# A graph network's first pair: filter taps of three outputs in two row groups of TensorE, and gates that begin with x and messages

## The chip, the core and the metric

The kernel runs on one core of one Trainium2 chip. The metric is the device time of one execution in microseconds, as the median of repeated runs. TensorE (PE, with its weight loads PEld) does the matrix products, VectorE (DVE), ScalarE (ACT) and GpSimd (POOL) the elementwise work, and SyncE (SP) issues nearly all DMA transfers. Every engine works through its own queue in order.

## The reference

There are 64 graphs of 256 nodes with 256 features each, all in fp32, and two layers. The first layer has a convolution branch of 17 taps along the nodes, a message branch and a gated unit that joins them:

```python
h = relu(bn1(conv1(xc)))                       # 1 tap, xc is x transposed
x_conv = relu(bn2(conv2(h)) + xc)              # 17 taps, 256 -> 256 channels
s = x @ w_se.T + b_se                          # 3 numbers per node
A = exp(-dist(s, s)) * adj
x_nmp = A @ relu(x @ w_msg.T + b_msg)          # messages
gi, gh = [x_conv, x_nmp] @ w_ih.T + b_ih, x @ w_hh.T + b_hh
r, z = sigmoid(gi_r + gh_r), sigmoid(gi_z + gh_z)
x = layernorm(x + (1 - z) * tanh(gi_n + r * gh_n) + z * x)
# layer 1
hn = layer_norm(x, gamma, beta)
x = layernorm(x + relu((adj @ hn) @ W_rel + b_rel + hn @ W_root))
```

## The kernel before

**Pairs and blocks.** Graphs are worked on in 32 pairs. Eight graphs, four pairs, share one block of the convolution. The convolution of 17 taps is a product of polynomials: DVE splits the inputs into 47 (`NM`) frequencies (`split_all`, `split_u`, `butterflies`, L679), TensorE multiplies each frequency by its own 256 x 256 matrix (`product`, L707), and DVE puts the results together again (`merges`, then L897 to L905), after which ACT scales them into `xc` (`kept`, L911). All of block b+1 is spread over the pairs of block b.

**The filters.** The 47 matrices `W2` are made at the start from the 17 taps of `conv2_w`, in `filters()`. Before the change POOL lays seven output channels (`OB = 7`) of 17 taps side by side in `ws` (`laid`, L542, one copy for four such blocks), TensorE transposes each block (`turned`, L548), ACT copies the result to `tT` (L550), TensorE multiplies it by a constant matrix `taps` of 119 rows and 329 columns (L565), and ACT writes the 329 columns to `W2` (L568), each with seven outputs of all 47 frequencies. The ring `ws` is four groups deep. Every frequency needs all outputs, so block 0's products (`products_added`, `last_products`) begin only when the filters are done. `W2` is stored to DRAM for the later blocks (`store_w2`), and the pool that holds it closes after block 0's last product. The gates' weights `WB` are loaded into the space that is then free (L1026).

**A pair.** `pair(p)` computes the messages (`ps_msg`, L1092, and L1095 which adds the bias in pairs 0 and 1 by a product of one row), the distances (`ps_dist`, L1125: four products of four rows each in row groups of their own and in four banks), the adjacency-weighted exponentials, the sum of the messages `nmp` (`ps_nmp`, L1139), adds x to `xc` (L1145, L1146), and then the gates. A gate bank holds 512 columns: half for r or z, half for a part of n. Most pairs use a form with seven products in place of eight; pairs 0, 1 and the last, `PLAIN`, use eight plain ones into `ps_g`. For pairs 0 and 1 a bank takes its eight products in two groups, one for each half of the features; each group takes x, xc and messages in this order:

```python
for f in range(C):
    for g in gs:
        a = bank("ps_g", "gate")
        for k in range(C):
            product(a, (f, k, g), T is ZN, k == 0)
        put(T, f, g, a)
```

Four of the eight PSUM banks may be held for gates, six for the rest. After the gates come the first norm, the projection (`ps_hy`, L1311), the aggregation (`ps_agg`, L1325), the last norm and the store.

**Small sums.** `beta`, two tiles of 128 columns, is made by DVE (L1042) and multiplied by the layer's weights (`ps_hrow`, L1045); the column means of the weights follow (`ps_mean`, L1054).

**The x loads.** From block 3 on (`TURN_FROM`) x is loaded in 32 x 32 blocks with a DMA for every four blocks (L799, sixteen DMAs for a pair), so that DVE can transpose it (L813).

**The order.** Every operation has a key, a due time. `scheduled()` plays the program with estimated durations and takes, for each engine, the ready operation with the smallest key; the order that comes out is each engine's queue. DVE operations of a pair get `PAIR_LEAD` taken from their keys. `FIRST_GATES` is the due time of pair 0's gates, `PERIOD` the step from pair to pair, `GATE_TIME` the time for half of the gates; `spread` gives the convolution and the filters keys between two times.

Of the kernel before, what the change touches and what calls it, by code (L numbers as in the profile page):

```python
# [18 lines left out]
P = 128  # L19
B, N, D = 64, 256, 256  # L20
C = D // P
# [30 lines left out]
NM = 3 * len(LEAVES) + 2  # L52
SR, LR = 32, 100
SQ = 32
OB = 7
HQ = 2 * M * C * (M + 1)
XC_SLOTS = BG + 2
FIRST_GATES, PERIOD, GATE_TIME = 143.0, 60.5, 17.0
AHEAD_FROM, AHEAD_TO, W_DEEP = -20.0, 10.0, 2
CONV1_FROM, CONV1_TO, CONV_FROM, CONV_OUT, CONV_TO = -10.0, 120.0, -6.0, -70.0, -30.0  # L60
PAIR_LEAD, FILTER_LEAD, LOAD_AHEAD = 20.0, 15.0, 12.0
SMALL_RUNS, TURN_FROM = 2.5, 3
PLAIN, SUMS_FROM = (0, 1, B // 2 - 1), 2


# [199 lines left out]
class Engine:  # L265
# [4 lines left out]
    def __getattr__(self, method):  # L270
        program, name = self.program, self.name

        def call(*args, hold=(), need=(), lines_up=0, **named):
# [12 lines left out]
            if method == "dma_start":  # L286
                v = outs[0] if isinstance(outs[0], View) else named["in_"]
                dur, moved = 0.06, v.size() * v.at.shape[0] * 4
                if program.joined is not None:
                    moved *= SMALL_RUNS  # L290
            elif name == "tensor":
                turned = method == "transpose" or named.get("is_transpose")
                dur = 0.109 if turned else 2 * max(0.109, n * 0.8333e-3 + 0.0025)
            elif name == "vector":
                dur = 0.182 if method == "bn_aggr" else 0.147 + 1.044e-3 * (args[1].size() if method == "bn_stats" else n)
                dur += 0.06 * (method == "scalar_tensor_tensor" and isinstance(args[2], View))
            elif name == "scalar":
                dur = 0.16 + 0.83e-3 * n + 0.11 * sum(isinstance(named.get(k), View) for k in ("bias", "scale"))
                dur += 0.2 * ("accum_out" in named)
                where = outs[0].at[0].ravel()  # L300
                dur += 0.9e-3 * n * (n > 1 and "accum_out" not in named and where[1] - where[0] > 1)
            else:
                dur = 1.5 if ALU.pow in args else 0.45 + 1.5e-3 * n
# [106 lines left out]
def gnn_two_layers(  # L410
# [65 lines left out]
    h_dram = tc.dram_tile([B // 2, 5, P, D], F32, name="hd")  # L476
    xt_dram = tc.dram_tile([B // 2, P, C, 2 * N], F32, name="xt")
    W2 = sb("w2all", [P, C, NM, D], "first")
    taps = sb("taps", [TAPS * OB, NM * OB], "filters")

    prog.at(0.0)
    A.dma_start(out=chan_sb, in_=chan)
    A.dma_start(out=w1, in_=w1T.rearrange("(c p) n -> p c n", p=P))
    tb = np.einsum("kf,op->kofp", tap_matrix(), np.eye(OB, dtype=np.float32)).reshape(TAPS * OB, NM * OB)
    A.dma_start(out=taps, in_=nc.inline_tensor(np.ascontiguousarray(tb), name="tap_matrix").ap())
    V.memset(mhalf, -0.5)
    V.memset(ones, 1.0)
# [25 lines left out]
            SP.dma_start(out=w2m[f:g, c].rearrange("f p o -> p f o"), in_=W2[:, c, f:g, :])  # L513

    def filters():
        pieces, groups = [], []
        for c in range(C):
            for o0, o1 in ((0, 12 * OB), (12 * OB, 24 * OB), (24 * OB, D)):
                starts = [min(o, D - OB) for o in range(o0, o1, OB)]
                for a in range(0, len(starts), 4):  # L520
                    groups.append((len(pieces), starts[a:a + 4]))
                pieces.append((c, o0, o1))
        WT, TT = {}, {}
        WS, AHEAD = {}, 4
        wts = ring("wt", [P, TAPS, D - 24 * OB], 2, "filters")
        wss = ring("ws", [P, 4, TAPS, OB], AHEAD, "filters")
        tTs = ring("tT", [TAPS * OB, 4, P], 2, "filters")

        def fetch(i):
            if i < len(pieces):  # L530
                c, o0, o1 = pieces[i]
                t = next(wts).rearrange("p k o -> p (k o)")[:, :TAPS * (o1 - o0)]
                WT[i] = t.rearrange("p (k o) -> p k o", k=TAPS)
                SP.dma_start(out=WT[i], in_=w2T[c, :, :, o0:o1])

        def laid(i):
            piece, starts = groups[i]
            n, o = len(starts), starts[0] - pieces[piece][1]
            if i == 0 or groups[i - 1][0] != piece:
                fetch(piece + 1)  # L540
            WS[i] = next(wss)
            G.tensor_copy(WS[i][:, :n], WT[piece][:, :, o:o + n * OB].rearrange("p k (b o) -> p b k o", o=OB))  # L542

        def turned(i):
            ps, n = bank("ps_tT"), len(groups[i][1])
            with prog.group():
                for k in range(n):
                    PE.transpose(ps[:TAPS * OB, k * P:(k + 1) * P], WS[i][:, k].rearrange("p k o -> p (k o)"), ident)  # L548
            tT = next(tTs)
            A.copy(tT[:, :n].rearrange("k b p -> k (b p)"), ps[:TAPS * OB, :n * P])  # L550
            return tT

        fetch(0)
        for i in range(AHEAD):
            laid(i)
        TT[0] = turned(0)
        for i, (piece, starts) in enumerate(groups):
            c = pieces[piece][0]
            if i + AHEAD < len(groups):
                laid(i + AHEAD)  # L560
            if i + 1 < len(groups):
                TT[i + 1] = turned(i + 1)
            for a, o in enumerate(starts):
                ps = bank("ps_w")
                PE.matmul(ps[:, :NM * OB], TT[i][:, a, :], taps, start=True, stop=True)  # L565
                skip = OB - D % OB if o == D - OB else 0
                pv = ps[:, :NM * OB].rearrange("p (f o) -> p f o", o=OB)
                A.copy(W2[:, c, :, o + skip:o + OB], pv[:, :, skip:])  # L568

    def sl(a, n, step=1):  # L570
        return X[:, a:a + n] if step == 1 else X[:, a:a + (n - 1) * step + 1:step]
# [212 lines left out]
    def conv1(b):  # L784
# [5 lines left out]
        def fetch(g):  # L790
            if b >= TURN_FROM:
                XN[g] = xn_ahead[:, :4 * D]
                blocks = XN[g].rearrange("p (c g b i) -> p g c b i", c=C, g=2, i=SQ)
                with prog.group():
                    for a in range(P // SQ):
                        for k in range(2):
                            for c in range(C):
                                at = c * P + a * SQ
                                SP.dma_start(out=blocks[a * SQ:(a + 1) * SQ, k, c], in_=x[b * BG + g + k][  # L799
                                    :, at:at + SQ].rearrange("(b j) i -> j b i", j=SQ))  # L800
                return
            if b > 0:
                XN[g] = xn_ahead[:, :4 * D].rearrange("p (j d) -> p j d", d=D)
# [134 lines left out]
    prog.lead = 0.0  # L938
    at3 = len(prog.ops)
    spread(at1, at2, 2.0, 14.0)  # L940
    spread(at2, at3, 12.0, 70.0)
    for o in prog.ops[at1:at3]:
        if o.moved:
            o.key = min(o.key, 20.0)
# [41 lines left out]
    G.tensor_sub(half_r, half_r, bhh[:, 2])  # L986
    G.tensor_scalar(half_r, half_r, 0.5, None, ALU.mult)

    prog.at(58.0, 0.01)
    store_w2(0)  # L990
    store_w2(1)

# [46 lines left out]
    beta = HY[:, 0, 0, :D].rearrange("p (c e) -> p c e", c=C)  # L1039
    ps = bank("ps_hrow")  # L1040
    for c in range(C):
        V.tensor_scalar(beta[:, c, :], ones, gb[:, 1, c:c + 1], None, ALU.mult)  # L1042
    with prog.group():
        for c in range(C):
            PE.matmul(ps, beta[:, c, :], wrr[:, c, :], start=(c == 0), stop=(c == C - 1))  # L1045
# [23 lines left out]
    def pair(p):  # L1069
# [79 lines left out]
        for v, t, when in zip(ins, (tx, nmps, tc_), (due - 28, due - 10, due - 20)):  # L1149
# [16 lines left out]
                V.tensor_sub(t3, b22, b12)  # L1166
            right.append((b11, b21, b22, t4, t1, t2, t3))

        def product(ps, i, second, start):
            gates = (((0, (0, 2, 1)), (2, (0,))), ((1, (0, 2, 1)), (2, (2, 1))))[second]  # L1170
            left, at = i, i
# [31 lines left out]
        if plain:  # L1203
            prog.at(due, 2 * GATE_TIME / 44)
            for gs in ((0,), (1,)) if apart else ((0, 1),):
                for T in (RG, ZN):
                    for f in range(C):
                        for g in gs:
                            a = bank("ps_g", "gate")
                            for k in range(C):  # L1210
                                product(a, (f, k, g), T is ZN, k == 0)
                            put(T, f, g, a)
                        squash(T, f, gs)
        else:
# [258 lines left out]
```

## Time and profile before

| | |
|---|---|
| median of 3 runs | 2065.92 us (2064.77 to 2066.36) |
| the profiled execution | 2065.45 us |
| its span, first to last instruction | 2063.7 us |
| granted TensorE clock, mean | 0.995 |
| PE, DVE, ACT, POOL busy | 98%, 81%, 51%, 14% |
| chain that ended last, by engine | PE 92%, DVE 5% |
| tap matmuls L565 | 24.0 to 72.0 us from the start |
| pair 0's gates, first `ps_g` matmul | 152.1 us |

The profile is of one execution. Its line for a group of instructions has the source line, engine, operation, tiles, shapes and count, then the busy time and the mean of one, then the idle time ahead of them and what ended it. An fp32 matmul appears as two MATMUL rows, so 74 tap matmuls are counted as 148. A table by stretches gives, for each stretch, the busy time and count of PE, PEld, DVE, ACT and POOL, then the granted clock (1.00 is full speed), the share of the DMA engines that was busy and the GB/s.

### The profile page before, as it was taken

Reading aid. Unit: us, or ns where it says so; the run is one execution under the profiler, and the core shown is the slowest. Engines: PE = TensorE matmul, PEld = TensorE weight load, DVE = VectorE, ACT = ScalarE, POOL = GpSimd, SP = SyncE. Lnnn points to the kernel's source line nnn. Section 1 sums busy time; section 2 is a strip of 40 time slices with the busy share of each in tenths; the row PEclk is TensorE's granted clock in tenths of the full one; section 3 lists DMA queues with packets and bytes.
Section 4 is the critical chain, followed back from the end, with each engine's and each line's share of the span. In section 5 each row is a group of like instructions: output and inputs, shape, how many; then the busy total and the mean of one; then the engine's idle time right before and its main releaser. Section 6 shows DMA issues by size and latency. Waiting matters only on the chain.

```text
span 2063.7 us, 28744 instructions
## 1 busy us (share of the span) xinstructions
PE 2029.6 (98%) x10332; PEld 1645.4 (80%) x10332; DVE 1678.4 (81%) x2587; ACT 1047.5 (51%) x2460; POOL 296.9 (14%) x520
## 2 busy tenths in 40 slices
PE   9989999999999999999999999999999999999997
PEld 6868779778887788877887778877888778887875
DVE  7983798899968998889968998799887899875644
ACT  7453534754446544565447544475445554465432
POOL 4010210111111111101101121112110111111100
PEclk9999999999999999999999999999999999999999
DMA  8834363334433264334532354333452224211100
GB/s 213 265 99 156 105 205 121 105 120 146 152 97 113 78 184 138 95 100 125 176 98 97 101 155 149 104 116 84 151 159 80 72 77 153 93 38 61 41 21 31
DMA packets 284683, 241.21 MB, mean 117 GB/s; under 512 B 110469, under 2 KB 269180, under 8 KB 284540
## 3 DMA queue, kind: packets, MB, share of 16 engines
q1 hardware_dynamic: 283998, 238.94, 37.8%
q8 instruction: 82, 1.34, 0.3%
q14 instruction: 61, 0.50, 0.1%
q10 hardware_dynamic: 542, 0.43, 0.1%
HBM read 177.85 MB, written 61.47 MB: 116 GB/s over the span
## 4 chain that ended last, share of the span: by engine, by line
PE 92%; DVE 5%; ACT 1%; issue 1%; POOL 0%; POOLq 0%; DVEq 0%; ACTq 0%
PE ps_a L1179 21%; PE ps_k L707 15%; PE ps_hy L1311 10%; PE ps_d L1179 10%; PE ps_msg L1092 5%; PE ps_agg L1325 5%; PE ps_b L1179 5%; PE ps_nmp L1139 5%; PE ps_c L847 5%; PE ps_g L1179 4%; PE ps_w L565 2%; PE ps_wT L1276 1%; DVE XF L679 1%; PE ps_dist L1125 1%; PE ps_tT L548 0%
## 5 line engine op out<-in xcount | busy, mean ns | idle before, releaser
L707 PEld LDWEIGHTS ps_k<-XF,cs 128*128 128x128 f32 x2632 | 316.3, 192 | 15.6 <-issue 9.6
L707 PE MATMUL ps_k<-XF,cs 128*128 128x128 f32 x2632 | 318.3, 275 | 0.0
L1311 PE MATMUL ps_hy<-wrr,wT 128*128 128x512 f32 x512 | 228.3, 593 | 1.5 <-ACT XF L724 1.5
L1179 PE MATMUL ps_a<-nmp,WB 128*128 128x256 f32 x696 | 207.5, 380 | 0.0
L1311 PEld LDWEIGHTS ps_hy<-wrr,wT 128*128 128x128 f32 x512 | 95.4, 190 | 103.0 <-issue 92.1
L1191 ACT COPY ZN<-ps_a 128x512 f32<-128x512 f32 x116 | 68.0, 586 | 194.1 <-PE ps_a L1179 193.8
L1179 PE MATMUL ps_a<-tx,WB 128*128 128x256 f32 x522 | 158.2, 385 | 0.2
L1193 ACT ACTIVATE RG<-ps_a,bhh 128x512 f32<-128x512 f32 x116 | 79.2, 683 | 139.9 <-PE ps_a L1179 107.2
L1179 PEld LDWEIGHTS ps_a<-nmp,WB 128*128 128x128 f32 x696 | 132.5, 190 | 18.3 <-ACT nmp L1141 0.2
L1335 ACT ACTIVATE HY<-HY 128x256 f32<-128x256 f32 x112 | 45.7, 408 | 177.9 <-DVE HY L1329 172.4
L1092 PE MATMUL ps_msg<-wms,xT 128*128 128x260 f32 x512 | 133.4, 383 | 0.0
L679 DVE TENSOR_TENSOR XF<-XF 128x512 f32<-128x512 f32 (+3 forms) x128 | 126.3, 1009 | 5.3 <-ACT XF L760 3.3
L1139 PE MATMUL ps_nmp<-AT,msg 128*128 128x256 f32 x512 | 120.6, 384 | 6.4 <-DVE AT L1132 6.2
L1313 DVE SCALAR_TENSOR_TENSOR HY<-ps_hy,q,hrow 128x512 f32<-128x512 f32 x128 | 95.4, 747 | 36.1 <-PE ps_hy L1311 31.8
L1325 PE MATMUL ps_agg<-HY,adja 128*128 128x256 f32 x512 | 120.1, 380 | 2.6 <-DVE HY L1313 2.6
L1325 PEld LDWEIGHTS ps_agg<-HY,adja 128*128 128x128 f32 x512 | 96.1, 190 | 29.5 <-issue 12.9
L1139 PEld LDWEIGHTS ps_nmp<-AT,msg 128*128 128x128 f32 x512 | 96.3, 192 | 21.9 <-DVE AT L1132 6.6
L1179 PEld LDWEIGHTS ps_a<-tx,WB 128*128 128x128 f32 x522 | 94.4, 191 | 21.2 <-issue 6.9
L847 PE MATMUL ps_c<-xTc,w 128*128 128x512 f32 x232 | 107.5, 594 | 1.4 <-ACT xTc L827 1.4
L1092 PEld LDWEIGHTS ps_msg<-wms,xT 128*128 128x128 f32 x512 | 93.4, 190 | 14.2 <-issue 1.8
L1179 PE MATMUL ps_a<-xc,WB 128*128 128x256 f32 x348 | 103.6, 379 | 0.8 <-ACT xc L1146 0.8
L1289 POOL TENSOR_SCALAR total<-total 128x4 f32<-128x4 f32 x28 | 13.5, 484 | 631.4 <-ACT x L1285 631.4
(205 smaller groups left out, 4519.7 us busy)
## 6 DMA issues: line engine op xcount, KB each, us to landing
cs<-w2m SPq DMA_DIRECT2D x105, 768.0 KB, 4.9
adjm<-in_adjT_dram SPq DMA_DIRECT2D x64, 256.0 KB, 2.8
xT<-xt SPq DMA_DIRECT2D x32, 512.0 KB, 3.9
adja<-in_adjT_dram SPq DMA_DIRECT2D x64, 256.0 KB, 2.7
out_dram<-HY SPq DMA_DIRECT2D x64, 256.0 KB, 2.1
hd<-xn SPq DMA_DIRECT2D x28, 544.0 KB, 3.3
XF<-hd SPq DMA_DIRECT2D x28, 544.0 KB, 4.2
xt<-xTc SPq DMA_DIRECT2D x29, 512.0 KB, 2.7
```

The source lines that it names most:

```text
L679: (V.tensor_add if add else V.tensor_sub)(sl(o, n), sl(a, n), sl(b, n))
L707: PE.matmul(ps[:, o * P:(o + 1) * P], w(m, c)[:, o * P:(o + 1) * P], X[:, slot, c * P:(c + 1) * P], start=first and o == 0 and c == 0, sto ...
L847: PE.matmul(ps, w1[:, c, o * P:(o + 1) * P], xTc[:, c, :], start=(c == 0), stop=(c == C - 1), hold=[h[:, :, o]])
L1092: PE.matmul(ps[:, :D + 4], xT[:, c, g, m * P:(m + 1) * P], wms[:, c, :], start=(c == 0), stop=(c == C - 1 and not idle), hold=[msg[:, g, m]])
L1139: PE.matmul(ps[:, d * N:(d + 1) * N], msg[:, g, m, d * P:(d + 1) * P], AT[:, g, m, :], start=(m == 0), stop=(m == C - 1), hold=[nmp[:, :, g]])
L1179: PE.matmul(ps[:, h * N:(h + 1) * N], block[:, s, gate, :], right[s][at], start=start and h == 0 and j == 0, stop=j == len(sources) - 1, s ...
L1191: A.copy(o, ps)
L1193: A.activation(o, ps, AF.Identity, bias=bhh[:, 2, f:f + 1])
L1311: PE.matmul(ps, wT[:, 2 * f + g, m * P:(m + 1) * P], wrr[:, f, :], start=(f == 0), stop=(f == C - 1), hold=[HY[:, g, m]], need=[] if apart ...
L1313: stt(HY[:, g, m, :], ps, q[:, 1, j:j + 1], hrow)
L1325: PE.matmul(ps[:, n_ * D:(n_ + 1) * D], adja[:, g, m, n_ * P:(n_ + 1) * P], HY[:, g, m, :D], start=(m == 0), stop=(m == C - 1))
L1335: A.activation(HY[:, g, m, :D], y[:, m, :], AF.Copy, accum_out=total[:, j:j + 1])
```

## The change

In `filters()` a block is now three output channels (`OB = 3`) of 17 taps, 51 rows. Two blocks stand side by side, one in partitions 0 to 63 and one in 64 to 127 (`OG = 64`), so that one transpose turns both. `taps` has its 51 rows of 141 columns twice, and two matmuls use one row group each and write to a bank each; three such pairs make a round of 18 outputs. A round has two POOL copies, three transposes, one copy to `tT`, six matmuls and two ACT writes of 423 columns. The padding of `ws` is set to zero once.

In pairs 0 and 1 a gate bank takes first all products of x and messages and then, as a group of its own, those of xc. In the last pair all three stay one group. `beta` is made by ACT. A pair's transposing x load is eight DMAs of both graphs instead of sixteen. Nearly all due times and leads have other numbers, and the estimate for a matmul of 51 or of 4 rows is smaller.

```diff
-OB = 7
+OB, OG = 3, 64
-FIRST_GATES, PERIOD, GATE_TIME = 143.0, 60.5, 17.0
-AHEAD_FROM, AHEAD_TO, W_DEEP = -20.0, 10.0, 2
-CONV1_FROM, CONV1_TO, CONV_FROM, CONV_OUT, CONV_TO = -10.0, 120.0, -6.0, -70.0, -30.0
-PAIR_LEAD, FILTER_LEAD, LOAD_AHEAD = 20.0, 15.0, 12.0
-SMALL_RUNS, TURN_FROM = 2.5, 3
+FIRST_GATES, PERIOD, GATE_TIME = 133.0, 60.0, 17.1
+AHEAD_FROM, AHEAD_TO, W_DEEP = -9.1, 12.4, 2
+CONV1_FROM, CONV1_TO, CONV_FROM, CONV_OUT, CONV_TO = -10.0, 120.0, -6.0, -70.0, -32.4
+PAIR_LEAD, FILTER_LEAD, LOAD_AHEAD = 40.4, 19.1, 9.6
+SMALL_RUNS, TURN_FROM = 1.3, 3
+FILTERS_TO, STORES_AT = 50.0, 54.5
...
+                if not turned:
+                    dur *= {51: 0.52, 4: 0.36}.get(args[1].at.shape[0], 1.0)
...
-        wss = ring("ws", [P, 4, TAPS, OB], AHEAD, "filters")
-        tTs = ring("tT", [TAPS * OB, 4, P], 2, "filters")
+        wss = ring("ws", [P, 3, 2, OG], AHEAD, "filters")
+        tTs = ring("tT", [P, 3, P], 2, "filters")
+        for _ in range(AHEAD):
+            G.memset(next(wss), 0.0)
...
-            G.tensor_copy(WS[i][:, :n], WT[piece][:, :, o:o + n * OB].rearrange("p k (b o) -> p b k o", o=OB))
+            for g in range(2):
+                at = o + g * n * OB
+                G.tensor_copy(WS[i][:, :n, g, :TAPS * OB].rearrange("p b (k o) -> p b k o", o=OB),
+                              WT[piece][:, :, at:at + n * OB].rearrange("p k (b o) -> p b k o", o=OB))
...
-            for a, o in enumerate(starts):
-                ps = bank("ps_w")
-                PE.matmul(ps[:, :NM * OB], TT[i][:, a, :], taps, start=True, stop=True)
-                skip = OB - D % OB if o == D - OB else 0
-                pv = ps[:, :NM * OB].rearrange("p (f o) -> p f o", o=OB)
-                A.copy(W2[:, c, :, o + skip:o + OB], pv[:, :, skip:])
+            pss, size = [bank("ps_w") for _ in range(2)], NM * OB
+            with prog.group():
+                for k in range(n):
+                    for g in range(2):
+                        r = slice(g * OG, g * OG + TAPS * OB)
+                        PE.matmul(pss[g][:, k * size:(k + 1) * size], TT[i][r, k, :], taps[r, :], start=k == 0,
+                                  stop=k == n - 1, skip_group_check=True)
+            for g in range(2):
+                first = o + g * n * OB
+                skip = max(0, done - first)
+                done = first + n * OB
+                pv = pss[g][:, :n * size].rearrange("p (b f o) -> p f b o", b=n, o=OB)
+                to = W2[:, c, :, first:done].rearrange("p f (b o) -> p f b o", o=OB)
+                A.copy(to[:, :, :, skip:], pv[:, :, :, skip:])
...
-                        for k in range(2):
-                            for c in range(C):
-                                at = c * P + a * SQ
-                                SP.dma_start(out=blocks[a * SQ:(a + 1) * SQ, k, c], in_=x[b * BG + g + k][
-                                    :, at:at + SQ].rearrange("(b j) i -> j b i", j=SQ))
+                        for c in range(C):
+                            at = c * P + a * SQ
+                            SP.dma_start(out=blocks[a * SQ:(a + 1) * SQ, c], in_=rows_of[:, :, at:at + SQ])
...
-    spread(at2, at3, 12.0, 70.0)
+    spread(at2, at3, 12.0, FILTERS_TO)
...
-    prog.at(58.0, 0.01)
+    prog.at(STORES_AT, 0.01)
...
-        V.tensor_scalar(beta[:, c, :], ones, gb[:, 1, c:c + 1], None, ALU.mult)
+        A.activation(beta[:, c, :], ones, AF.Identity, scale=gb[:, 1, c:c + 1])
...
+        def products_of(ps, f, g, second, ks):
+            gates = (((0, (0, 2, 1)), (2, (0,))), ((1, (0, 2, 1)), (2, (2, 1))))[second]
+            with prog.group():
+                for h, (gate, sources) in enumerate(gates):
+                    for s in (s for s in sources if s in ks):
+                        for k in range(C):
+                            left = (0, 1, 6, 3)[2 * f + k]
+                            block = A21[0] if left == 6 else WB[:, left]
+                            PE.matmul(ps[:, h * N:(h + 1) * N], block[:, s, gate, :], right[s][2 * k + g],
+                                      start=0 in ks and h == 0 and s == sources[0] and k == 0,
+                                      stop=s == sources[-1] and k == C - 1, skip_group_check=True)
...
-                            for k in range(C):
-                                product(a, (f, k, g), T is ZN, k == 0)
+                            for ks in ((0, 1), (2,)) if not apart else ((0, 1, 2),):
+                                products_of(a, f, g, T is ZN, ks)
```

## The prediction

> **What bounds the kernel now.** I read the page first, then the busy time by stretches, TensorE's waits, the groups of the filter stage, and short pieces of the chain and of the timeline.
>
> ```profile
> span 2063.7 us, 28744 instructions
> PE 2029.6 (98%) x10332; PEld 1645.4 (80%) x10332; DVE 1678.4 (81%) x2587; ACT 1047.5 (51%) x2460; POOL 296.9 (14%) x520
> ```
>
> TensorE is busy for 98%; what can be won is its work or its few holes. The stretches (busy PE, PEld, DVE, ACT, POOL, then the granted clock) say where the holes are:
>
> ```profile
> 24.00:72.00 48.00, 48.00 (x213) 34.97 (x212) 46.24 (x54) 42.05 (x93) 15.91 (x19) 1.00 0.70 202
> 72.00:137.40 65.40, 65.16 (x468) 55.83 (x467) 55.86 (x89) 21.49 (x46) 5.60 (x12) 1.00 0.54 171
> 137.40:152.30 14.90, 7.32 (x18) 2.83 (x18) 12.32 (x21) 11.06 (x16) 0.00 (x0) 0.73 0.41 148
> ...
> 160.00:2040.00 1880.00, 1867.18 (x9473) 1524.26 (x9473) 1534.07 (x2360) 950.41 (x2265) 264.90 (x461) 1.00 0.37 112
> ```
>
> 24 to 72 is the filter stage, full on PE, with DVE (46.2 of 48) and ACT (42.1) close behind. 72 to 137.4 holds block 0's products and the messages. 137.4 to 152.3 is the one large hole, with a reduced clock. From 160 to 2040 PE is idle for 12.8 us in all, so a start that ends earlier ends the kernel earlier by about as much. What makes the hole:
>
> ```profile
> PE ps_hrow L1045 <- DVE HY L1042: 6.3, 1, 6.3
> PE ps_mean L1054 <- DVE wrr L1050: 1.3, 2, 1.0
> ```
>
> ```profile
> 143.67 3.80 PE ps_hrow L1045 x4
> ...
> 152.26 4.69 PE ps_g L1179 x16
> ...
> 164.72 15.32 PE ps_g L1179 x71
> ```
>
> PE's queue holds the beta product (L1045) ahead of pair 0's gates; its input is queued on DVE behind the last recombinations (L905, to 143.4). The gates want xc, whose second ACT step (L1146) ends at 151.3. Four passes of 512 columns take 3.80 us here, and 16 gate passes 4.69, where 71 take 15.32 later (0.216 each).
>
> **The filter stage, part A.** The groups of 24 to 72:
>
> ```profile
> L565 PE MATMUL ps_w<-taps,tT 119*128 119x329 f32 x148 | 43.7, 440 | 0.0
> L568 ACT COPY w2all<-ps_w 128x329 f32<-128x329 f32 x72 | 32.6, 459 | 4.7 <-PE ps_w L565 0.4
> L542 POOL COPY ws<-wt 128x476 f32<-128x476 f32 x12 | 11.3, 953 | 18.7 <-PE ps_tT L548 15.8 <-DMA wt<-in_w2T_dram 2.9
> ```
>
> Each matmul is two passes. The chain gives 2.22 us for 8 passes of 329 columns (0.277 each) and 0.44 for four transposes; a group of 28 outputs is 2.66 us of PE.
>
> PE after: a round of 18 outputs is 3 transposes (0.33) and 12 passes of 141 columns, by columns 0.120 each. Serial they are 1.44, in two overlapping rows 0.72. That rows overlap, the chain shows at the distances: 8 passes of 256 columns in four row groups take 0.64 us, serial 1.73. Leaving the full array and coming back costs too: the two one-row passes of the messages (L1095, 260 columns) take 0.63 us where the four before them take 0.88, so 0.19 per excursion. A round is 0.33 + 0.72 + 0.19 = 1.24 us, 28 rounds and two small ones (0.55) 36 us against 48; without overlap 1.96 a round, 56.
>
> ACT after: four evictions of 329 in 1.73 us when ACT is late (25.15) are 0.426 apart. 94 columns more at 0.84 ns (L759, 256 columns, 0.37; L737, 512, 0.59) make 0.505; 56 of them 28.3, 28 copies tT of 384 columns at 0.45 12.6, the small rounds 1.6: 42.5 us. So ACT allows 5.5 us less than now.
>
> POOL after: 60 copies of 153 elements instead of 20 of 476 (the same elements). Three copies that follow each other beside a full DVE:
>
> ```profile
> 47.45 3.18 POOL L542 COPY ws<-wt 128x476 f32<-128x476 f32 x3 [1.92 <-PE ps_tT L548]
> ```
>
> ```profile
> 48.12 1.00 DVE L612 SCALAR_TENSOR_TENSOR XF<-XF 128x512 f32<-128x512 f32 x1
> 49.04 1.11 DVE L610 SCALAR_TENSOR_TENSOR XF<-XF 128x512 f32<-128x512 f32 x1
> 50.18 0.99 DVE L612 SCALAR_TENSOR_TENSOR XF<-XF 128x512 f32<-128x512 f32 x1
> ```
>
> One copy passes for each DVE instruction, and delays it (1.0 for 0.69). The small copy of 119 elements issued at 58.66 also ends only at 59.31, after DVE's instruction ends at 59.17, and delays nothing visible. So small copies still wait for DVE's boundaries. Eight copies are made ahead, 52 remain, and DVE has 54 instructions in the 48 us: at one each, 46.2 us. POOL, not PE, sets this stage. With a drain of the last round I take -1 us. Ends: -5.5 (ACT alone) and +8.5 (rows do not overlap). The four memsets of the ring fall into POOL's idle 8.95 us before 14.6: 0, at most 4 x 0.29 without that cover. DVE's delay goes with elements: 0; if it went with copies, 40 x 0.3 = 12 us on DVE, which is full here. The products that follow find V0's inputs early (sums from 56), so PE is next.
>
> The Trainium skill, "TensorEngine Tiling (Array Packing)", Tiling Modes, says that switching the tiling mode drains TensorE, which speaks against two switches a round; the 0.19 us row is that price. Its Performance Considerations say that tiling does not speed up the PSUM copies; by that rule alone the stage would end by ACT, a forecast nearer to 2050.
>
> **Pair 0's gates, part B.** In 137.4 to 152.3 PE does 4 + 4 passes of 512 columns (0.43 each) and the distances: 4.1 us of full-speed work, so 10.8 lost; the 16 gate passes lose 4.69 - 3.46 = 1.2. Together 12.0 us. The change puts x and messages of a bank ahead of xc: for r's four banks 12 passes each, 48 x 0.216 = 10.4 us of work that needs no xc. Its inputs: messages' sum nmp from 122.6; WB's loads, issued 127.3 to 135.2 and 4.1 us each, in by 139. So 4.1 + 10.4 = 14.5 of 14.9 us fill, and the clock has no idle to fall in. xc itself gets no later. I take -11; the ends are 0 (the order still puts L1045 first) and -12.0. Behind the early parts, xc parts wait with four gate banks held; nobody else takes that share before z's gates.
>
> The beta rows go from DVE (0.48 us) to ACT, two copies of 128 columns, at most 0.3 each: off L1045's DVE queue, but possibly ahead of xc's L911 on ACT: 0 to +0.6; taken 0.
>
> **x loads and constants, part C.** Half of the 320 transposing x loads (0.45 us of SP each) go, with the same bytes; SP spends long waits for buffers and no PE wait leads to these loads: 0, the ends -1 and +1.
>
> New due times and leads re-order DVE, ACT and SP everywhere; no row shows that. Below: the 12.8 us of idle between 160 and 2040 could vanish. Above: see the slow rival. Taken 0, as PE's total is unchanged there.
>
> Sum: -1 - 11 + 0 = -12 us. The profiled execution is 2065.45 (span 2063.7 and 1.75 around it), so 2053.4; the median shown is 0.5 higher: 2054.
>
> **A clock rule.** After a wait of 2.66 us at 1890 the granted clock is 0.50 until about 1899; so the rounds beside DVE's 2.3 to 2.7 us instructions (53.9 to 61.5) may cost up to 3 us of it, which lies inside part A's upper end. The Trainium skill, "TensorE: Matmul & The Clock Gate", Part 1, puts the re-throttle after an idle window of about 3.4 us; the row shows it sooner. By the page, the short gaps between rounds would cost no clock and the sum would stay as it is.
>
> **The rivals.** Filter stage shorter too: POOL's small copies slip between DVE's instructions, ACT sets the pace, A = -5.5, and 2049. For it: 0.51 us for the copy of 119 at 34.11. Against: the 3.18 us row. Chance 0.15.
>
> Filter stage longer: POOL gets less than one copy per DVE instruction around L679 (2.3 to 2.7 us each) or rows overlap poorly, A = +8.5: 2063.5; half of that, 2059. Chance 0.17.
>
> Slower: the doubled pair lead on DVE. Pair work goes ahead of the convolution's (28 of 30 us busy through the blocks), so the next block's sums come late and PE starves at each of seven block boundaries. The chain passes over DVE's L679 at 1190 and 1434 already, three of 2.3 us each time. If each boundary pays 2.5 us (the idle there now), +17.5 outweighs -12 and gives 2071.5; from 1.7 us a boundary on it decides. Against: PE at 30.00 of 30 in most stretches. Chance 0.15.
>
> The change does not do what it says: L1045 still stands first in PE's queue, B = 0, 2065. Chance 0.05.
>
> **How the numbers follow.** The main case, 2050 to 2058, has 0.48. 2046 to 2066 leaves out the slow rival and the end of the short one, under 0.2. A difference of 0.2%, 4.1 us, is about what a measurement of this kernel can tell from none. Faster by more: 0.48 + 0.15 + two thirds of 0.17 + 0.02 = 0.76; within: the rest of the long stage and of the failed one, 0.09; slower: 0.15.
>
> **What would show it.** Right: ps_w in pairs of rows, filters ending near 71 with ACT waiting for PE and PE for POOL's ws; ps_g on x and nmp before 145, no 6.3 us wait at L1045, clock 1.0 from 137 to 155. Wrong: first products before 68 or after 76; ps_g still starting near 150; PE idle from 160 to 2040 far from 12.8 us.

## The result, and the profile after

The changed kernel takes 2085.65 us (median of 4 runs, 2082.47 to 2087.06), the kernel before 2065.74 (2064.77 to 2066.36): a ratio of 1.010, 95% interval 1.0087 to 1.0112. The forecast was 2054, with a range of 2046 to 2066. The change makes the kernel 20 us slower.

The page's first lines of the kernel after:

```profile
span 2085.2 us, 29031 instructions
PE 2044.9 (98%) x10540; PEld 1662.2 (80%) x10540; DVE 1677.2 (80%) x2585; ACT 1044.6 (50%) x2458; POOL 324.4 (16%) x564
```

PE's busy time grew by 15 us, although tap products were to overlap. The busy times by stretches (PE, PEld, DVE, ACT, POOL, then the granted clock, DMA share, GB/s):

```profile
24.00:62.00 38.00, 31.27 (x249) 24.94 (x248) 36.12 (x39) 22.72 (x53) 31.42 (x32) 0.73 0.39 87
62.00:92.00 30.00, 30.00 (x182) 23.73 (x183) 16.38 (x28) 16.48 (x38) 11.64 (x22) 0.50 0.70 228
92.00:150.00 58.00, 58.00 (x436) 52.94 (x435) 40.23 (x62) 15.81 (x33) 2.86 (x5) 0.97 0.46 152
150.00:165.00 15.00, 14.76 (x56) 9.28 (x57) 14.55 (x24) 10.62 (x20) 2.93 (x7) 1.00 0.74 232
165.00:2060.00 1895.00, 1878.61 (x9511) 1531.01 (x9509) 1550.21 (x2383) 961.50 (x2284) 263.87 (x463) 1.00 0.37 112
```

The filter stage has two halves. To 62 us PE is busy 31 of 38 at a clock of 0.73, beside a full DVE (36.1). From 62 to 92 PE is busy without a break, but at 0.50, while DVE, ACT and POOL have time to spare. The last eviction ends at 91.9; before it was 72.3. The hole ahead of pair 0's gates is gone: 14.76 of 15 us are busy at a clock of 1.00.

TensorE's waits from 24 to 92 (us in total, times, longest), then pieces of its timeline (start, us, line, count, idle before it and its releaser):

```profile
PE ps_tT L559 <- POOL ws L552: 6.4, 5, 2.0
PE ps_w L581 <- ACT tT L561: 0.3, 1, 0.3
```

```profile
25.50 0.55 PE L559 MATMUL ps_tT<-ident,ws 128*128 128x128 f32 x3
25.98 0.99 PE L581 MATMUL ps_w<-taps,tT 51*128 51x141 f32 x12
26.90 1.53 PE L559 MATMUL ps_tT<-ident,ws 128*128 128x128 f32 x12
...
32.24 0.55 PE L559 MATMUL ps_tT<-ident,ws 128*128 128x128 f32 x3 [2.00 <-POOL ws L552]
32.72 0.99 PE L581 MATMUL ps_w<-taps,tT 51*128 51x141 f32 x12
34.79 0.90 PE L559 MATMUL ps_tT<-ident,ws 128*128 128x128 f32 x3 [1.08 <-POOL ws L552]
...
66.09 0.90 PE L559 MATMUL ps_tT<-ident,ws 128*128 128x128 f32 x3
66.92 1.78 PE L581 MATMUL ps_w<-taps,tT 51*128 51x141 f32 x12
68.63 0.90 PE L559 MATMUL ps_tT<-ident,ws 128*128 128x128 f32 x3
```

A round takes 1.40 us at full clock (25.50 to 26.90). Two waits for POOL, 2.00 and 1.08 us, are followed by transposes at half speed. Behind a short return to full clock and two more such waits (1.18 and 1.81 us, to 61.0), nearly every round takes 2.54 us (66.09 to 68.63) with no wait between them. By the clock's record it is 0.50 from 34.5 to 51.6 and from 58.4 to 95.9. Each length in it is a multiple of 3.4 us.

What POOL and DVE did ahead of the first fall, from their timelines:

```profile
26.19 8.54 POOL L552 COPY ws<-wt 128x153 f32<-128x153 f32 x8 [2.86 <-PE ps_tT L559]
```

```profile
28.08 1.36 DVE L618 SCALAR_TENSOR_TENSOR XF<-XF 128x1024 f32<-128x1024 f32 x1
29.36 1.35 DVE L620 SCALAR_TENSOR_TENSOR XF<-XF 128x1024 f32<-128x1024 f32 x1
30.75 1.24 DVE L631 SCALAR_TENSOR_TENSOR XF<-XF 128x1024 f32<-128x1024 f32 x1
```

POOL makes one copy in 1.07 us on average, and in 1.28 us beside these DVE instructions, one for each. A round needs two copies, so POOL feeds a round in some 2.1 to 2.6 us where PE needs 1.40.

Pair 0's gates, from the timeline:

```profile
152.19 1.98 PE L1065 MATMUL ps_hrow<-wrr,HY 128*128 128x512 f32 x4
...
160.70 1.03 PE L1197 MATMUL ps_g<-xT,WB 128*128 128x256 f32 x4
...
172.78 3.62 PE L1197 MATMUL ps_g<-xc,WB 128*128 128x256 f32 x16
```

The parts of x and messages run first, xc's last, and the wait of 6.3 us at the beta product is gone. All of it merely lies some 21 us too late: in run e1 below, the same kernel with the filters of before, the first gates start at 139.2 and the first products of xc at 151.6.

### The profile page after: what moved, and what is told of

Its sections match the earlier page's. It is cut to its first block, busy times and chain, and to the rows that moved or that the text cites. A ratio compares the mean times of both kernels' runs of the same rounds, so it can differ in the third digit from the quotient of the medians.

```text
span 2085.2 us, 29031 instructions
## 1 busy us (share of the span) xinstructions
PE 2044.9 (98%) x10540; PEld 1662.2 (80%) x10540; DVE 1677.2 (80%) x2585; ACT 1044.6 (50%) x2458; POOL 324.4 (16%) x564
## 4 chain that ended last, share of the span: by engine, by line
PE 92%; DVE 5%; issue 1%; ACT 1%; POOL 0%; DMA 0%; SPq 0%; POOLq 0%; ACTq 0%; DVEq 0%
PE ps_a L1211 21%; PE ps_k L728 16%; PE ps_d L1211 11%; PE ps_hy L1343 10%; PE ps_agg L1357 5%; PE ps_msg L1112 5%; PE ps_c L867 5%; PE ps_b L1211 5%; PE ps_nmp L1159 4%; PE ps_g L1197 4%; PE ps_w L581 2%; PE ps_wT L1308 1%; PE ps_dist L1145 1%; PE ps_tT L559 1%; DVE XF L633 1%
## 5 line engine op out<-in xcount | busy, mean ns | idle before, releaser
L1343 PEld LDWEIGHTS ps_hy<-wrr,wT 128*128 128x128 f32 x512 | 95.4, 190 | 99.0 <-issue 92.5
L1357 PEld LDWEIGHTS ps_agg<-HY,adja 128*128 128x128 f32 x512 | 97.2, 192 | 33.6 <-issue 21.5
L1211 PEld LDWEIGHTS ps_a<-tx,WB 128*128 128x128 f32 x522 | 94.3, 191 | 24.7 <-issue 10.1
L1211 PE MATMUL ps_a<-tc,WB 128*128 128x256 f32 x348 | 104.0, 380 | 0.0
```

What stands on the lines that cost most here:

```text
L1211: PE.matmul(ps[:, h * N:(h + 1) * N], block[:, s, gate, :], right[s][at], start=start and h == 0 and j == 0, stop=j == len(sources) - 1, s ...
L1343: PE.matmul(ps, wT[:, 2 * f + g, m * P:(m + 1) * P], wrr[:, f, :], start=(f == 0), stop=(f == C - 1), hold=[HY[:, g, m]], need=[] if apart ...
L1357: PE.matmul(ps[:, n_ * D:(n_ + 1) * D], adja[:, g, m, n_ * P:(n_ + 1) * P], HY[:, g, m, :D], start=(m == 0), stop=(m == C - 1))
```

## The experiments

The medians, each beside runs of the kernel before on the same chip; where there is no interval, it is one run. "Filters" is the end of the last eviction of taps, "pair 0" the start of pair 0's projection (`ps_hy`), "last" the time from the last pair's projection to the end, all in us of the profiled execution. "Pair 0" compares only kernels that have the same order: in the kernel before and in e2 that projection stands later in PE's queue. The equal numbers of before and after do not mean equal progress (pair 2's projection starts at 374.7 and 391.8).

| run | us | before | ratio (95%) | filters | pair 0 | last |
|---|---|---|---|---|---|---|
| before | | | | 72.3 | 222.0 | 26.0 |
| after | 2085.65 | 2065.74 | 1.0087 to 1.0112 | 91.9 | 221.7 | 28.9 |
| e1 old filters | 2068.15 | 2064.73 | 1.0009 to 1.0028 | 73.4 | 200.5 | 28.9 |
| e2 only new filters | 2084.88 | 2064.73 | 1.0083 to 1.0116 | 91.1 | 241.8 | 25.6 |
| e3 only the gates | 2061.82 | 2064.73 | 0.9973 to 0.9992 | 73.3 | 199.5 | 28.9 |
| e4 one copy a round | 2069.35 | 2064.73 | 1.0011 to 1.0030 | 65.9 | 199.9 | 28.9 |
| e5 more full products | 2077.68 | 2064.52 | | 80.0 | 208.6 | 28.9 |
| e7 gates, last pair as before | 2056.24 | 2064.52 | 0.9947 to 0.9972 | 72.7 | 198.9 | 25.6 |
| e8 e7 and one-copy filters | 2061.03 | 2064.82 | 0.9972 to 0.9990 | 65.8 | 201.6 | 26.0 |
| e9 old filters, old times | 2067.93 | 2064.52 | 1.0006 to 1.0025 | 73.4 | 200.5 | 28.9 |
| e11 e7 and beta on ACT | 2058.37 | 2064.82 | 0.9953 to 0.9976 | 72.8 | 199.5 | 25.6 |
| e12 e7 and 4-row estimate | 2072.15 | 2064.82 | 1.0022 to 1.0048 | 72.4 | 198.7 | 34.8 |
| e15 after, estimate and last pair undone | 2074.37 | 2064.16 | 1.0028 to 1.0057 | 90.2 | 217.3 | 25.6 |
| e16 e15 and one copy a round | 2058.12 | 2064.16 | 0.9957 to 0.9979 | 65.4 | 198.9 | 25.6 |

**Which part costs it.** Three kernels: after with the filters of before (e1), before with the new filters and the estimate for 51 rows (e2), before with the regrouped gates (e3, the last pair's included).

> The changed kernel with the filters of before (blocks of seven outputs, one row group), all else as changed: gates, loads, beta and due times. Theory 1 (the whole loss is the filter stage in two row groups, which runs at a granted clock of 0.50 for 17 and 37 us and ends at 91.9 us instead of 72.3): filters end near 72 with the clock at 1.00 and the time is about 2085.7 - 19.6 = 2066. Theory 2 (the new due times lose it in the blocks and at the end): 2078 or more. If the early gates earn what was forecast and nothing is given back: 2054.

> The kernel of before with the filters in two row groups alone; its due times, gates and loads stay. Theory 1 (filter stage): the clock falls to 0.50 within the stage, filters end 15 to 20 us later, and the time is 2081 to 2086. Theory 2 (due times): within 5 us of before, 2061 to 2071.

> The kernel of before with the gates of pairs 0 and 1 begun by x and messages alone. If the early parts fill the hole before 152 us as forecast: ps_g begins near 140 and the time is about 2055. If TensorE's queue still has the beta product first, or the gain is given back in block 1: 2063 to 2067.

The new filters alone make the kernel before 20.2 us slower, and without them the changed kernel is 17.5 us faster. Their stretches in e2, columns as above:

```profile
24.00:62.00 38.00, 35.36 (x244) 28.37 (x242) 35.98 (x39) 22.04 (x51) 31.26 (x32) 0.60 0.41 88
62.00:92.00 30.00, 29.73 (x199) 23.00 (x198) 15.98 (x28) 17.27 (x40) 11.79 (x22) 0.60 0.72 229
```

The order of everything else is another one, the loss the same. The gates alone gain 2.9 us.

**Is it the waits for POOL?** e4 makes both halves of `ws` with one copy (the blocks of the two row groups alternate), half as many instructions and the same elements (the transposes also take their `tT` buffer ahead of time, and the ACT writes follow the new order of the blocks):

```diff
-            for g in range(2):
-                G.tensor_copy(WS[i][:, :n, g, :TAPS * OB]...   # 128 x 153
+            G.tensor_copy(WS[i][:, :n].rearrange("p b g e -> p (b g) e")[:, :, :TAPS * OB]...   # 128 x 306
```

e5 leaves the copies and gives PE more to do, two useless products of 128 rows after each round's transposes:

```diff
                     PE.transpose(ps[:, k * P:(k + 1) * P], WS[i][:, k]..., ident)
+                for k in range(2):
+                    PE.matmul(ps[:, 3 * P:], ones, ones, start=True, stop=True)
```

> The changed kernel with one GpSimd copy of 306 elements for a round in place of two of 153 (the six blocks of a round lie alternately in the two halves; transposes take a tT buffer ahead). Theory 1a (GpSimd's two copies, one per VectorE instruction, make TensorE wait 6.4 us, the waits drop the clock, and only then is TensorE slow): the waits go, the clock stays at 1.00, filters end at 66 to 72, the time is 2060 to 2066. Theory 1b (the products in row groups do not keep the clock up by themselves): the clock is at 0.50 for most of the stage again, filters end at 85 or later, 2078 or more.

> The changed kernel with two more full 128-row products of 128 columns (four passes, 0.44 us at full clock, 0.88 at half) after each round's transposes, their result unused. If work in row groups holds a fallen clock down and full work lifts it: the clock falls at the same waits near 34 us but comes back within 7 us, filters end at 80 to 88 although TensorE does more, and the time is 2074 to 2082. If the clock is down for another reason (TensorE's waits alone): 0.50 for most of the stage, rounds of 3.4 us, filters end after 105, the time is over 2098.

Stretches of e4 and its wait for `ws`, then a stretch of e5:

```profile
28.00:35.00 7.00, 7.00 (x79) 5.46 (x78) 6.93 (x6) 7.00 (x16) 4.96 (x6) 1.00 0.80 179
35.00:52.00 17.00, 16.44 (x178) 12.67 (x174) 16.72 (x22) 16.18 (x38) 14.46 (x18) 1.00 0.52 123
52.00:65.00 13.00, 12.87 (x141) 9.94 (x138) 12.83 (x10) 13.00 (x29) 5.98 (x6) 1.00 1.06 365
```

```profile
PE ps_tT L557 <- POOL ws L550: 0.4, 1, 0.4
```

```profile
24.00:80.00 56.00, 53.42 (x546) 45.36 (x544) 52.53 (x66) 40.51 (x92) 43.91 (x53) 1.00 0.64 182
```

With one copy a round TensorE waits 0.4 us for `ws` in all, the clock stays at 1.00, ACT is full, and the filters end at 65.9, 26 us sooner than in the changed kernel. With more work on PE (1.84 us a round) the clock stays too, and the filters end 12 us sooner than with less work. So the waits cost the time by way of the clock: of themselves they sum to 6.4 us.

**What does the clock count?** e6 appends stretches of useless products to the kernel before: full rows, two groups of 51 rows, one group of 51, two of 64, four of 32, transposes, and rounds like those of the filters.

> The kernel of before with TensorE work of no use behind its end: stretches of 60 products (two passes of 128 columns each, in a queue without waits) in one row group of 51 rows, in two, in two of 64, in four of 32, of transposes, and rounds of three transposes and three pairs of 51 rows, each stretch between full 128-row stretches of 60 products. Theory 1b (row-group products do not count as full work for the clock): the clock falls to 0.50 a few us into the stretches of 51 rows, though the queue has no wait, and comes back in the full ones. Theory 1a (only waits drop it): 1.00 through all stretches, 13 us for a full or a paired one.

From its timeline:

```profile
2066.82 13.67 PE L1404 MATMUL ps_x<-ones 51*128 51x128 f32 x240
2080.42 13.66 PE L1397 MATMUL ps_x<-ones 128*128 128x128 f32 x120
2094.01 13.66 PE L1404 MATMUL ps_x<-ones 51*128 51x128 f32 x120
2107.61 15.29 PE L1397 MATMUL ps_x<-ones 128*128 128x128 f32 x120
```

Two row groups do 240 passes in the time of 120: they overlap fully, and the clock stays at 1.00. Behind 13.66 us of one row group alone it is 0.50, from 2107.8 for 3.4 us. Transposes (60 in 6.71 us) and rounds (1.35 us each) do not. e10 was to try the return from 0.50 behind pauses:

> The kernel of before with TensorE work of no use behind its end, each stretch after a pause of some 14 us in which VectorE alone works, so that each begins at a granted clock of 0.50: 120 full products, 120 pairs in two groups of 51 rows, 18 rounds of three transposes and three such pairs, 160 transposes, 18 rounds with two full products more in each, 120 products in four groups of 32 rows. If work in row groups cannot lift a fallen clock: the full stretch and the rounds with full products come to 1.00 within 7 us, and the pairs, the rounds and the four groups stay at 0.50 to their end (27, 46 and 27 us). If any work without waits lifts it: all come to 1.00 within 7 us.

The order put its stretches among the last pair's work, PE was warm for nearly all of them (1.00 from 1861 on), and it answers nothing on the return.

**What brings the clock back?** Four stretches put into the changed kernel itself, ahead of the taps of round 21, where it runs at 0.50:

```diff
             with prog.group():
+                for _ in range(30 if i == 21 else 0):
+                    PE.matmul(pss[0][:, :P], ones, ones, start=True, stop=True, skip_group_check=True)
                 for k in range(n):
```

e13 has 30 full products, e14 30 pairs of 51 rows, e17 90 transposes, e18 ten rounds of 3 transposes and 3 pairs.

> The kernel after the change, with 30 useless products of 128 rows and 128 columns inserted ahead of the taps of round 21, which lies at about 69 us in the kernel after, where the granted clock is 0.50 and PE is busy without a pause. Theory A (rounds in two row groups are not counted as full work by the clock, full products are): the clock returns to 1.00 within some 7 us of the stretch, the stretch takes well under 13.6 us, and the seven large rounds behind it run at 1.40 us each instead of 2.54, so that the first product of block 0 comes only about 2 us after the 91.2 of the kernel after. Rival B (the clock returns by its own calendar, some 35 us after the last pause, whatever PE does): the stretch takes 13.6 us throughout at half clock and the filters end near 105.

> The same, but the stretch consists of 30 pairs of products of 51 rows in two row groups, which took as long as 30 full ones when both ran at full clock. Theory A: the stretch stays at half clock for its whole 13.6 us, as the rounds do, and the filters end near 105 us, some 11 us later than with full products. Rival C (any dense queue without waits brings the clock back): it comes back inside this stretch too and both runs end alike.

> The kernel after the change with 90 useless transposes of a 128 x 128 tile at the place where the two runs before had products (clock 0.50, about 70 us). Full products brought the clock back 1.1 us into their stretch, pairs of row groups 6.8 us. If transposes are what the clock doesn't count, it stays at 0.50 through the whole stretch, which then takes about 20 us (60 took 6.71 at full clock). If any dense queue counts, it is back within 7 us and the stretch takes 12 to 14 us.

> The same with ten rounds of 3 transposes and 3 pairs of products of 51 rows that wait for nothing, the mix of the filter stage without its waits for the POOL and ACT copies. If the mix itself is what holds the clock down (a third of the time in transposes, two changes between full array and row groups a round), it stays at 0.50 and the stretch takes about 24 us. If the small waits for the copies in the real rounds hold it down, it comes back within some 7 us and the stretch takes under 17 us.

Each stretch in its run's timeline (of e18 the products during which the clock returns, and the next transposes):

```profile
67.96 7.40 PE L579 MATMUL ps_w<-ones 128*128 128x128 f32 x60
```

```profile
71.97 10.22 PE L581 MATMUL ps_w<-ones 51*128 51x128 f32 x120
```

```profile
71.71 11.34 PE L580 MATMUL ps_w<-ident,ones 128*128 128x128 f32 x90
```

```profile
68.43 1.37 PE L583 MATMUL ps_w<-ones 51*128 51x128 f32 x12
69.72 0.55 PE L580 MATMUL ps_w<-ident,ones 128*128 128x128 f32 x3
```

The clock returns at 69.1, 78.8, 74.5 and 69.4: 1.1, 6.8, 2.8 and 1.8 us into the stretch. After that the real rounds keep it. All four are single runs, at 2077.15, 2076.95, 2083.97 and 2081.93 us, which is 13.0, 12.8, 21.2 and 19.2 above the kernel before on their own chips, where the changed kernel is 19.9 above: 7 to 14 us of useless work cost next to nothing, and in e13 and e14 they save some 7 us. So neither row groups nor transposes are uncounted; theory A falls as it stands, and rival B too. In e2 and e15 the real rounds even brought the clock back by themselves (86.1 and 84.4 us, after 55 and 51).

What keeps the real rounds at 0.50 for 30 us can be read from the traces. The clock changes only at steps of 3.41 us. For each such window I add up the columns that TensorE's passes stream (0.842 ns a column at full clock, from the 0.277 us for 329 columns, and twice that at 0.50), each pass weighted by its rows out of 128; the sum as a share of the window is its fill. The twenty traces have 12,129 such whole windows (without the first 8 us and the last window of each):

| clock in the window | changed after it | changed only at a fill | always changed at a fill |
|---|---|---|---|
| 1.00 | fell 94 times | up to 0.39 | below 0.36 |
| 0.50 | returned 76 times | from 0.73 up | above 0.79 |

Busy time, or passes counted without their rows, do not separate the windows like this.

A real round at half clock fills 0.70 of its time: 3 transposes of 128 columns and 12 passes of 141 columns at 51 of 128 rows are worth 1058 full columns, 1.78 of 2.54 us. At full clock the same round fills 0.64. So rounds can hold a clock of 1.00, and can hardly win it back. The falls in the changed kernel follow windows of 0.26 and 0.37, and from 61.8 to 92.5 its windows lie at 0.68 to 0.76. The window in which the clock came back had 0.83 in e13, 0.81 in e14 and 0.995 in e17. In e18, e2 and e15 it had 0.75 to 0.77, where the changed kernel twice stayed at 0.50: there the return is luck, and e18 shows nothing of its stretch. The one row group of e6 fills 0.38, just where the clock may fall. This account is worked out from the traces of runs made for other questions. No run tested its lines on purpose, and the stretches also differ from the rounds in having operands of ones.

**The gates and the last pair.** e7 takes the regrouping for pairs 0 and 1 alone (against e3, shortened):

```diff
-                            for ks in ((0, 1), (2,)) if not apart else ((0, 1, 2),):
-                                products_of(a, f, g, T is ZN, ks)
+                            if apart:      # the last pair, as before
+                                for k in range(C): product(a, (f, k, g), T is ZN, k == 0)
+                            else:
+                                for ks in ((0, 1), (2,)): products_of(a, f, g, T is ZN, ks)
```

> The kernel of before with the gates of pairs 0 and 1 begun by x and messages, the last pair's products grouped by feature halves as before. The run with the last pair regrouped too took 2061.8, and its last stretch, from the last pair's projection on, 28.9 us instead of 26.0. If the regrouping of the last pair costs that: 2059, 0.3% below before. If those 2.9 us come from elsewhere: 2062.

2056.24: 8.3 us faster than before, 5.6 faster than e3, and the best kernel of the study. The old hole in e7, then two of its waits:

```profile
138.00:153.00 15.00, 14.34 (x63) 11.56 (x62) 14.14 (x21) 12.09 (x15) 0.00 (x0) 1.00 0.39 146
```

```profile
PE ps_agg L1341 <- DVE HY L1329: 2.6, 2, 2.2
PE ps_wT L1292 <- DVE wT L1271: 0.6, 1, 0.6
```

In e3 (and, to the digit, in the kernel after) the last pair has this instead:

```profile
PE ps_agg L1337 <- issue: 6.5, 1, 6.5
PE ps_wT L1288 <- DVE sh L1310: 0.9, 1, 0.9
```

Before, gate products of the last pair still run between its first and second projection (L1179 at 2039.4 to 2041.5 in the kernel before), with work for PE while the norm is made. In the kernel after the gates end at 2056.0 and the first projection starts at 2056.3, and PE stands for 6.5 us before the last aggregation.

**Due times, beta, the estimate.** e9 is e1 with the due times of before as well; e11 is e7 with beta on ACT; e12 is e7 with the planner's shorter estimate for 4-row products (the distances), which changes the order and no instruction.

> The changed kernel with the filters and all due times, leads and gaps of before; gates, beta on ScalarE, merged x loads and the estimate for four rows stay as changed. The gates alone took 2061.8, the changed kernel with old filters 2068.2. If the due times cost the 6.3 us between them: 2062 here. If beta or the merged loads cost them: 2067 to 2069.

> The kernel with the gates of pairs 0 and 1 alone (2056.2) and beta made by ScalarE. Beta, the merged x loads and the estimate for four rows cost some 6 us between them. If it is beta, which lets the small sums go ahead of the first gates: 2061 to 2063. If not: 2055 to 2057.

> The kernel with the gates of pairs 0 and 1 alone (2056.2) and the smaller estimate for products of four rows, which moves the distances in every queue and changes no operation. If the estimate costs the 6 us: 2061 to 2063. If not: 2055 to 2057.

The due times are worth nothing that shows (2068.15 against 2067.93). Beta on ACT is 2.1 us above e7 with intervals that overlap. The estimate costs 15.9 us against e7. The merged x loads were not run alone. Waits of e12 in the last stretch:

```profile
PE ps_agg L1343 <- DVE HY L1331: 6.4, 1, 6.4
PE ps_wT L1294 <- DVE wT L1273: 3.0, 1, 3.0
```

The last stretch has 9.2 of them (34.8 against 25.6); the rest has gathered before (pair 24's projection at 1684.4 against 1674.1, the last pair's at 2036.3 against 2028.4).

**Mended.** e8 adds the one-copy filters to e7. e15 is the changed kernel without the 4-row estimate and with the last pair as before. e16 is e15 with one copy a round.

> The due times of before, the gates of pairs 0 and 1 begun by x and messages, and the filters in two row groups with one GpSimd copy a round. The same with the filters of before took 2056.2. If the clock stays at 1.00 and the earlier end of the filters (66 us) reaches the gates: 2050. If VectorE's chain to xc sets pair 0's gates whatever the filters do: 2055 to 2058.

> The kernel after the change with its new filters, beta, loads and due times, but without the shorter estimate for matmuls of 4 rows and with the last pair's gates in the order of before. If these two cost in the changed kernel what they cost beside the other orders (5.6 us for the last pair; 16 us for the estimate alone, about 6 with the last pair regrouped), it takes 2074 to 2080 us, and the filters still end near 91. If the estimate costs nothing among the new due times: 2080. If the filters alone explain the loss: 2085.

> As the run before, with the filters of one POOL copy a round as well, so that the clock stays at 1.00 through the filter stage and the filters end at 66 us. From 2069.35 us (one copy alone) less 5.6 for the last pair and less the estimate's share: 2058 to 2064. If the earlier filters help at all, it falls under the 2056.24 of the kernel with early gates alone; if xc, which DVE sets, still comes at 151 us, it does not.

e15 takes back 10 of the 20 us (each held against the kernel before on its own chip), e16 another 16. But e16 is level with e7 (the intervals overlap) and e8 is above it: filters that end 7 us sooner bring pair 0's projection to 198.9 and 201.6, where e7 has it at 198.9. The stretch behind the filters shows where the gain stays. First e16, then e7:

```profile
65.00:130.00 65.00, 63.60 (x452) 55.68 (x450) 59.33 (x97) 17.57 (x40) 3.02 (x5) 0.97 0.52 170
130.00:150.00 20.00, 18.80 (x79) 13.90 (x80) 18.99 (x28) 16.04 (x24) 2.67 (x7) 1.00 0.56 182
```

```profile
72.00:130.00 58.00, 58.00 (x444) 52.25 (x442) 48.39 (x78) 16.72 (x36) 2.85 (x5) 1.00 0.47 157
130.00:150.00 20.00, 19.57 (x79) 13.60 (x78) 19.62 (x28) 14.69 (x23) 2.74 (x7) 1.00 0.66 216
```

DVE is at 95% and more from 130 to 150 in both, and xc's second ACT step ends at 148.0 and 151.6, so half of the 7.3 us by which the filters end sooner is gone there already. PE reaches that point earlier in e16 and waits: it is idle for 4.8 us and at half clock for 10.2 between the filters' end and pair 0's projection, against 1.5 and 0 in e7.

## Why the prediction was wrong

**Part A, the filter stage, is the step that failed:** -1 us was forecast, with ends of -5.5 and +8.5; alone it measured +20.2, in the changed kernel 16.3 (e15 against e16). Its pieces were nearly right. Rows do overlap. PE's round is 1.40 us where 1.24 was worked out: two changes between the full array and row groups cost about 0.3 us a round, not 0.19. POOL does pass about one copy per DVE instruction. Two steps were not. First, 52 copies over 54 DVE instructions gave 46.2 us "at one each", an average over the stage. But DVE's instructions last 1.2 to 2.7 us in some parts and 0.4 to 0.8 in others: rounds starve at first, and POOL waits for PE later (12.6 us in 24 to 92). Second, the clock: "up to 3 us of it, which lies inside part A's upper end". The waits that the first step hides lower the clock for 51 us of the stage, and then the sentence "POOL, not PE, sets this stage" is false: at 2.54 us a round PE sets it, and at a fill of 0.70 it does not win the clock back. The page's rule that was weighed there, the Trainium skill's "TensorE: Matmul & The Clock Gate", Part 1, has the clock fall after an idle window of about 3.4 us and return after one busy window of that length. The runs agree with the grid of 3.4 us. They do not agree with the rest: it fell after waits of 2.00 and 1.08 us with a round between them, in a window still filled to 0.26, and it stayed at 0.50 through 30 us in which PE showed no idle time. The forecast saw the row (2.66 us at 1890) and priced one fall, not a stage whose own rounds hardly climb out.

The other page weighed there, "TensorEngine Tiling (Array Packing)", Tiling Modes, says that a change of tiling mode drains the array. The runs show a price: e6's rounds with two changes take 1.35 us at full clock, where 3 of its transposes (0.34) and 12 of its passes in two groups (0.68) make 1.02, so some 0.33 us a round is an estimate of it.

**Part B, the gates, held in its mechanism.** The hole was to yield 11 of 12 us. In e7 PE's idle time ahead of pair 0's projection falls from 7.8 to 1.5 us and the time at half clock from 10.2 to 0, which is 6.3 and half of the 7.5 us that PE was busy at half clock, 10.1 us in all. At the end 8.3 arrive; where the rest goes was not followed. In the kernel after the hole is filled too (the stretch from 150 to 165).

**What was counted at nothing.** "In the last pair all three stay one group" was told as if nothing moved there: it costs 5.6 us (e3 against e7). The due times were taken at 0 and are 0. But the estimate for 4 rows, which issues nothing and was not priced at all, costs 15.9 us beside e7; together with the last pair it is 11.3 us inside the changed kernel (e15), or 9.7 when each run is held against its own kernel before, less than the sum of both alone. The other changes in e16, against before, give -6.0.

So the sum is: -6.0 for the mended change, +11.3 for estimate and last pair, +16.3 for the second copy with its clock, together +21.5 against 19.9 measured; the kernel before differs by 1.6 us between the two sets of runs. The three terms are differences along one row of runs, so that they add up confirms nothing.

**The rivals.** "Filter stage longer" had the right place and, at +8.5, half of the size. The slower rival had the right sign for another reason: its block boundaries are not where the time went (PE 1878.61 of 1895 us busy from 165 to 2060, 16.4 idle against 12.8), and the doubled lead cost nothing (e9).

## What to carry to other kernels

Where TensorE is fed by a slower engine, do not compare sums over a stage: take the stretch with the slowest feeder and ask whether PE is dense there, for short waits can cost the clock, and that is more than the waits. Work in row groups of 51 rows fills less of the array than it looks busy, and may then not win the clock back. When an edit also changes a planner's estimate, price the new order as a change of its own; an estimate alone moved this kernel by 16 us. And a stage that ends sooner is worth nothing until the chain behind it (here DVE's recombinations and xc) does too.

## What the runs showed of the hardware

- Adding work can be faster: two more full products a round ended the filters 12 us sooner (e5), and a stretch of 30 useless products in the slow stage made the run some 7 us shorter than the changed kernel (e13).
- Two row groups of 51 rows do 240 passes in 13.67 us, 120 full passes take 13.66: the overlap is complete, and the clock stays. One such group alone lost the clock at the end of its 13.66 us.
- The clock went by windows of 3.41 us and by the rows and columns in use: over 12,129 windows it fell only at a fill up to 0.39 and returned only from 0.73 on.
- The Trainium skill's "TensorE: Matmul & The Clock Gate", Part 4, says that transposes don't raise the clock as products do. Here 90 of them at 0.50 saw it return after 2.8 us, in a window that they filled to 0.995, and 60 in a row kept it at 1.00.
